# A four-layer graph network on one Trainium2 core: layer 0's graph part issued from a planned list, its second weight product in seven-product form

## The chip, the cores and the metric

The kernel runs on one core of one Trainium2 chip. The core has five engines with an instruction queue each: TensorE (PE in the profile, with its weight loads shown apart as PEld), VectorE (DVE), ScalarE (ACT), GpSimd (POOL) and SyncE (SP), which here only starts DMAs. Each engine takes its instructions in order, and waits for the others through semaphores. The metric is the device time of one execution in microseconds, the median of several runs. All arithmetic is float32.

## The reference

The input `x` is 128 sequences of 64 rows with 256 features, so 8192 rows; `adj` is one 64x64 matrix for all sequences. Four layers follow each other, each as `x = x + layer(relu(layernorm(x)))`. The change is in layer 0 alone:

```python
h = jnp.maximum(_layernorm(x, axis=-1), 0.0)
# the graph part of layer 0
h = jax.nn.relu(jnp.einsum('ts,bsh->bth', adj, h @ Wg0 + bg0))
h = jax.nn.relu(jnp.einsum('ts,bsh->bth', adj, h @ Wg1 + bg1))
# then, for p = 1..4, an LSTM over windows of p rows rewrites every p-th row of h
x = x + h
```

Layer 1 is a graph product with two weight products and batch norms, layer 2 three weight products on three parts of `adj`, layer 3 attention within each sequence. They stay as they are.

## The kernel before, in words

The 8192 rows are cut into 16 supertiles of 512 rows (`SUP`; `Q` = 4 blocks of `P` = 128 rows, two sequences each). `graph_part(s)` (from L277) is a generator that does one supertile in five stages, with a `yield` between them:

- load `xt` (one DMA of 512 KB, four of 128 KB for the first supertile), layer norm and ReLU to `h`: statistics on DVE (`norm_of`, L181 to L185), a power on POOL in their midst (L184), four activations on ACT (L191)
- `aggregate` to `g0`: 8 matmuls of 128x128 against the block-diagonal adjacency `adjT_bd` (L207), two PSUM copies on DVE (L208)
- the first weight product: 8 matmuls with 256 moving columns (L303), two additions of the bias on DVE (L305), one ReLU on ACT (L307), to `h1`
- `aggregate` to `g1`: as above, from `h1`
- the second weight product: for each of two output halves `o` two matmuls with 512 moving columns (L314), one bias operation on DVE (L317), one ReLU on ACT (L320), which writes transposed features into `hT`, the input of the LSTM

`pipelined(..., 1)` starts a new supertile every round and runs one stage of each live supertile a round, the youngest supertile first. The order of issue on each engine is just the order of these calls: in each round the load and layer norm of one supertile, `g0` of the one before, the first weight product of the next older, then `g1`, then the second weight product. Nothing is reordered afterwards (`manual_schedule`); an engine's queue is the order of the program.

Other work rides on the same stages: `row_sums` with supertile 0 (L129 to L133), `more_constants` with supertile 2 (weights and biases by DMA), `adjacencies` with 4, `normalize` with 7, and `weight_sums` (four POOL additions on LSTM weights, L267 to L270) with 9.

The LSTM that follows is written in another way. Its `at(t, fn)` puts every instruction with a due time by hand into a list `events`, and the list is sorted and issued. Its products use a seven-product form of a 2x2 block product (a Winograd form of Strassen): weights as `A11, A12, A21, A22` with the sums `S1` to `S4` made once, the moving side as two halves of columns with the sums `tx`, and results added up in PSUM banks named a, b and c. Its tiles come from the pools `lg`, `lh0` and `lh1`, opened after the graph part's pools `pa` and `pax` are closed, in the same memory. A pool opened with `reuse_waits="tile"` waits tile by tile for the older users of its memory; without it, it waits for all of them together. PSUM has 8 banks in one rotating pool (`bank()`).

Of the kernel before, what the change touches and what calls it, by code (L numbers as in the profile page):

```python
# [9 lines left out]
F32 = mybir.dt.float32  # L10
AF = mybir.ActivationFunctionType
ALU = mybir.AluOpType
AX = mybir.AxisListType

P = 128
# [5 lines left out]
def kernel(ctx: ExitStack, tc: tile.TileContext, a: dict, out: bass.AP):  # L21
# [48 lines left out]
    def bank():  # L70
        return psum.tile([P, 512], F32, tag="ps", name="ps")
# [11 lines left out]
    def weight(name, src, pool=const, queue=nc.sync):  # L83
        k, m = src.shape
        return load_const(name, src.rearrange("(c p) m -> p c m", p=P), [P, k // P, m], pool, queue)
# [21 lines left out]
    con = {}  # L107

    def more_constants():
        con["wg1"] = weight("wg1", a["Wg1"], first)  # L110
        con["bg1"] = load_const("bg1", a["bg1"], [P, KC], first)
        con["bih"] = load_const("bih", a["bih"], [P, NL, NM])
        con["bhh"] = load_const("bhh", a["bhh"], [P, NL, NM])
        con["bn1"] = load_const("bn1", a["bn1"], [P, 3, HC])
        con["bn2"] = load_const("bn2", a["bn2"], [P, 3, KC])
        con["w1"] = weight("w1", a["W1T"])
# [10 lines left out]
    def row_sums():  # L127

        nc.vector.reduce_sum(rs_col, adj_bd, axis=AX.X)  # L129
        nc.vector.tensor_scalar_mul(rsb, bg0, rs_col)  # L130
        ps = bank()
        nc.tensor.matmul(ps[:, :P], ones, adjT_bd, start=True, stop=True)
        nc.vector.tensor_copy(rs_row, ps[:, :P])  # L133

    def adjacencies():

        nc.vector.tensor_add(lbias, con["bih"], con["bhh"])


        scr = first.tile([P, P], F32, tag="scr", name="scr")  # L140
        nc.vector.tensor_add(scr, adj_bd, ident)
        nc.vector.reduce_sum(deg[:, 0:1], scr, axis=AX.X)
        nc.vector.tensor_mul(scr, scr, ident)
        nc.vector.reduce_sum(deg[:, 1:2], scr, axis=AX.X)
        nc.vector.tensor_add(ahT, adjT_bd, ident)
        nc.vector.reduce_sum(deg[:, 2:3], ahT, axis=AX.X)
        nc.vector.tensor_add(deg[:, 0:1], deg[:, 0:1], deg[:, 2:3])
        nc.vector.tensor_sub(deg[:, 0:1], deg[:, 0:1], deg[:, 1:2])
        nc.gpsimd.tensor_tensor(deg[:, 3:4], deg[:, 0:1], mhalf[:, 0:1], ALU.pow)
        dd = first.tile([P, P], F32, tag="dd", name="dd")  # L150
        nc.vector.tensor_scalar_mul(dd, ident, deg[:, 3:4])


        nc.vector.tensor_mul(adj3[:, 0, :], adjT_bd, ident)
        nc.gpsimd.affine_select(adj3[:, 1, :], adjT_bd, pattern=[[-1, P]], base=0,
                                channel_multiplier=1, compare_op=ALU.is_gt, fill=0.0)
        nc.gpsimd.affine_select(adj3[:, 2, :], adjT_bd, pattern=[[1, P]], base=0,
                                channel_multiplier=-1, compare_op=ALU.is_gt, fill=0.0)


        nc.gpsimd.affine_select(smask, adj_bd, pattern=[[-1, P]], base=0, channel_multiplier=1,
                                compare_op=ALU.is_ge, fill=NEG)
        nc.vector.memset(smask[T:P, 0:T], NEG)
        return dd

    def normalize(dd):
        ps = bank()
        nc.tensor.matmul(ps[:, :P], ones, dd, start=True, stop=True)
        nc.vector.scalar_tensor_tensor(ahT, ahT, deg[:, 3:4], ps[:, :P], op0=ALU.mult, op1=ALU.mult)


    def bcast_q(t):
        return t[:, None, :].to_broadcast([P, Q, t.shape[1]])
# [20 lines left out]
    def layernorm_relu(pool, src, tag="ln_h", bufs=None):  # L194

        rn = norm_of(pool, src)
        h = pool.tile([P, Q, D], F32, tag=tag, name=tag, bufs=bufs)
        normalize_relu(h, src, rn)
        return h

    def aggregate(pool, h, mT, tag, bufs=None):

        g = pool.tile([P, KC, SUP], F32, tag=tag, name=tag, bufs=bufs)
        for c in range(KC):
            p_ = bank()
            for q in range(Q):
                nc.tensor.matmul(p_[:, ts(q, P)], h[:, q, ts(c, P)], mT, start=True, stop=True)  # L207
            nc.vector.tensor_copy(g[:, c, :], p_)  # L208
        return g
# [18 lines left out]
    def graphs(s, c):  # L228

        v = hT[s // SG][:, c, :].rearrange("p (t b) -> p b t", b=GB)  # L230
        b = (s % SG) * (SUP // T)
        return v[:, b : b + SUP // T, :]

    def pipelined(gens, skew, live=()):


        gens, live, r = list(gens), list(live), 0
        while gens or live:
            if gens and r % skew == 0:
                live.insert(0, gens.pop(0))  # L240
            live = [g for g in live if next(g, "end") != "end"]
            r += 1
# [14 lines left out]
    def load_lstm(src, tag, pool):  # L257
        w = pool.tile([P, 7, 4, P], F32, tag=tag, name=tag)
        v = src.rearrange("(c p) (g h m) -> h c p g m", p=P, g=4, m=P)
        for h in range(2):  # L260
            for c in range(2):
                nc.sync.dma_start(w[:, 2 * h + c], v[h, c])
        return w

    def weight_sums(w):
        g = nc.gpsimd
        g.tensor_add(w[:, S1], w[:, A21], w[:, A22])  # L267
        g.tensor_sub(w[:, S2], w[:, S1], w[:, A11])
        g.tensor_sub(w[:, S3], w[:, A11], w[:, A21])
        g.tensor_sub(w[:, S4], w[:, A12], w[:, S2])  # L270

    GATES = (("i", 0, AF.Sigmoid), ("g", 2, AF.Tanh), ("f", 1, AF.Sigmoid), ("o", 3, AF.Sigmoid))


    with tc.tile_pool(name="pa", bufs=2) as pa, tc.tile_pool(name="pax", bufs=3) as pax:

        def graph_part(s):  # L277
            xt = pax.tile([P, Q, D], F32, tag="xt", name="xt")
            if s == 5:
                wih0.append(load_lstm(a["WihT"][0], "wih", lwa))  # L280
            for q in range(Q if s == 0 else 1):
                part = slice(q, q + 1 if s == 0 else Q)
                nc.sync.dma_start(xt[:, part, :], x_r[s, :, part, :])
            if s == 2:
                more_constants()
            h = layernorm_relu(pa, xt)
            if s == 0:
                row_sums()
            if s == 4:
                made.append(adjacencies())  # L290
            if s == 7:
                normalize(made[0])
            if s == 9:
                weight_sums(wih0[0])
            yield
            g0 = aggregate(pa, h, adjT_bd, "g0")
            yield
            h1 = pa.tile([P, Q, D], F32, tag="h1", name="h1")
            for q2 in range(0, Q, 2):
                p_ = bank().rearrange("p (q d) -> p q d", q=2)  # L300
                for q in range(2):
                    for c in range(KC):
                        nc.tensor.matmul(p_[:, q, :], g0[:, c, ts(q2 + q, P)], wg0[:, c, :],  # L303
                                         start=(c == 0), stop=(c == KC - 1))
                nc.vector.tensor_add(h1[:, q2 : q2 + 2, :], p_,  # L305
                                     rsb[:, None, :].to_broadcast([P, 2, D]))
            nc.scalar.activation(h1, h1, AF.Relu)  # L307
            yield
            g1 = aggregate(pa, h1, adjT_bd, "g1")
            yield  # L310
            for o in range(KC):
                p_ = bank()
                for c in range(KC):
                    nc.tensor.matmul(p_, con["wg1"][:, c, ts(o, P)], g1[:, c, :],  # L314
                                     start=(c == 0), stop=(c == KC - 1))
                t = pa.tile([P, SUP], F32, tag="h2", name="h2")
                nc.vector.scalar_tensor_tensor(  # L317
                    t.rearrange("p (q n) -> p q n", q=Q), bcast_q(rs_row), con["bg1"][:, o : o + 1],
                    p_.rearrange("p (q n) -> p q n", q=Q), op0=ALU.mult, op1=ALU.add)
                nc.scalar.activation(graphs(s, o), t.rearrange("p (b t) -> p b t", t=T), AF.Relu)  # L320
            yield

        wih0, made = [], []
        pipelined(map(graph_part, range(NS)), 1)
    graph_weights.close()


# [45 lines left out]
        yield  # L373


    lg = lstm.enter_context(tc.tile_pool(name="lg", bufs=1))

    lh1 = lstm.enter_context(tc.tile_pool(name="lh1", bufs=1))
    even_state = ExitStack()
    lh0 = even_state.enter_context(tc.tile_pool(name="lh0", bufs=1))  # L380
    events = []

    def at(t, fn, *args):
        events.append((t, len(events), fn, args))
# [514 lines left out]
```

## Time and profile before

| what | value |
|---|---|
| median of 6 runs | 1917.87 us (1914.57 to 1918.6) |
| the profiled execution: its own time / its span | 1916.72 us / 1915.0 us |
| mean granted TensorE clock | 0.996 |
| graph part: first aggregation to first LSTM product | 8.68 us to 182.65 us of the span |
| DMA over the span | 54.28 MB, mean 28 GB/s |

The table of slices (40 equal parts of the span) shows which engine is full where; a digit is the busy share in tenths, 9 meaning 90% or more. The first four columns are the graph part:

```profile
## 2 busy tenths in 40 slices
PE   7999999999999999999999999999999899999998
PEld 6776444444445666665444444555444788888886
DVE  6775777734546445445633334688786456565554
ACT  3554666534435435434533333444574333333332
POOL 1110322443424432322522224533152211111110
```

All times below are from the start of the span. In the profile a float32 matmul is two records, each with its weight load; records overlap, so a record's duration is longer than the distance from one to the next.

### The profile page before, as it was taken

What the parts mean: (1) busy time and instruction counts of PE and PEld (TensorE: products, weight loads), DVE (VectorE), ACT (ScalarE), POOL (GpSimd) and SP (SyncE); (2) the same over time, 40 slices, a digit from 0 to 9 for tenths busy, and PEclk for the clock granted to TensorE, in tenths of its full rate; (3) what the DMA queues carried; (4) which work ended last, traced back from release to release, by engine and by line L of the source; (5) the groups of instructions that cost most, each with busy time, mean ns of one, the idle gap of its engine ahead of it and who ended that gap; (6) DMA issues with size and microseconds to landing.
All of it is one profiled execution on the core that took longest, in us unless ns stands there. A gap on an engine that the chain in (4) does not pass through costs nothing.

```text
span 1915.0 us, 18932 instructions
## 1 busy us (share of the span) xinstructions
PE 1883.5 (98%) x6932; PEld 1147.5 (60%) x6932; DVE 1098.8 (57%) x2144; ACT 849.1 (44%) x1429; POOL 552.2 (29%) x363
## 2 busy tenths in 40 slices
PE   7999999999999999999999999999999899999998
PEld 6776444444445666665444444555444788888886
DVE  6775777734546445445633334688786456565554
ACT  3554666534435435434533333444574333333332
POOL 1110322443424432322522224533152211111110
PEclk9999999999999999999999999999999899999999
DMA  4110000100001000000000001233200001110111
GB/s 137 56 55 1 1 1 10 34 0 0 0 1 45 1 1 0 1 1 23 0 0 1 1 0 44 77 110 110 64 0 31 25 23 45 45 45 23 44 34 45
DMA packets 49469, 54.28 MB, mean 28 GB/s; under 512 B 3040, under 2 KB 44768, under 8 KB 49376
## 3 DMA queue, kind: packets, MB, share of 16 engines
q1 hardware_dynamic: 48640, 52.61, 8.8%
q8 instruction: 55, 0.90, 0.2%
q10 hardware_dynamic: 736, 0.46, 0.1%
q14 instruction: 38, 0.31, 0.1%
HBM read 36.28 MB, written 16.78 MB: 28 GB/s over the span
## 4 chain that ended last, share of the span: by engine, by line
PE 95%; DVE 2%; POOL 1%; ACT 1%; issue 1%; DMA 0%; SPq 0%; DVEq 0%; ACTq 0%; POOLq 0%
PE ps L449 34%; PE ps L455 19%; PE ps L796 9%; PE ps L365 6%; PE ps L684 5%; PE ps L207 4%; PE ps L303 3%; PE ps L822 3%; PE ps L314 3%; PE ps L814 3%; PE ps L783 2%; PE ps L830 1%; PE ps L217 1%; PE ps L851 1%; PE ps L807 1%
## 5 line engine op out<-in xcount | busy, mean ns | idle before, releaser
L471 DVE TENSOR_TENSOR gate<-gate,ps 128x512 f32<-128x512 f32 (+2 forms) x378 | 223.9, 619 | 446.4 <-PE ps L455 367.0
L449 PE MATMUL ps<-tx,wih 128*128 128x512 f32 (+2 forms) x1008 | 446.5, 542 | 3.1 <-issue 1.2
L449 PE MATMUL ps<-hT,wih 128*128 128x512 f32 (+2 forms) x756 | 338.5, 541 | 0.0
L449 PEld LDWEIGHTS ps<-tx,wih 128*128 128x128 f32 x1008 | 190.6, 190 | 193.0 <-issue 133.4
L474 ACT COPY gate<-ps 128x512 f32<-128x512 f32 (+2 forms) x252 | 134.2, 533 | 379.1 <-PE ps L455 325.2
L467 ACT ACTIVATE gate<-gate,lbias 128x512 f32<-128x512 f32 (+2 forms) x252 | 216.7, 860 | 158.0 <-DVE gate L471 158.0
L455 PE MATMUL ps<-h,whh 128*128 128x512 f32 (+2 forms) x576 | 256.6, 527 | 0.0
L449 PEld LDWEIGHTS ps<-hT,wih 128*128 128x128 f32 x756 | 143.6, 190 | 141.6 <-issue 79.9
L184 POOL TENSOR_TENSOR ln_rn<-ln_rn,mhalf 128x4 f32<-128x4 f32 x64 | 64.7, 1011 | 514.4 <-DVE ln_rn L183 514.4
L455 PE MATMUL ps<-th,whh 128*128 128x512 f32 (+2 forms) x432 | 192.5, 527 | 0.0
L796 PE MATMUL ps<-wl,ag 128*128 128x256 f32 x768 | 169.5, 381 | 0.0
L455 PEld LDWEIGHTS ps<-h,whh 128*128 128x128 f32 x576 | 109.4, 190 | 100.2 <-issue 76.5
L494 POOL TENSOR_TENSOR gate<-gate 128x1024 f32<-128x1024 f32 (+2 forms) x36 | 71.9, 2019 | 304.7 <-ACT gate L467 304.7
L796 PEld LDWEIGHTS ps<-wl,ag 128*128 128x128 f32 x768 | 145.7, 191 | 19.4
L191 ACT ACTIVATE ln_h<-x,ln_rn 128x256 f32<-128x256 f32 x128 | 66.4, 589 | 201.7 <-DVE ln_rn L185 201.7
L494 POOL TENSOR_TENSOR cell<-gate 128x1024 f32<-128x1024 f32 (+2 forms) x36 | 79.4, 2228 | 200.1 <-ACT gate L467 200.1
L455 PEld LDWEIGHTS ps<-th,whh 128*128 128x128 f32 x432 | 82.1, 190 | 75.2 <-issue 57.4
L365 PE MATMUL ps<-ag,w 128*128 128x512 f32 x256 | 112.3, 592 | 0.0
L494 POOL TENSOR_TENSOR cell<-gate,cell 128x1024 f32<-128x1024 f32 (+2 forms) x32 | 65.1, 2052 | 109.3 <-ACT gate L467 109.3
L474 DVE COPY gate<-ps 128x512 f32<-128x512 f32 (+2 forms) x126 | 78.5, 623 | 20.9 <-PE ps L455 20.8
L467 ACT ACTIVATE gate<-ps,lbias 128x512 f32<-128x512 f32 (+2 forms) x126 | 79.5, 631 | 3.9 <-PE ps L455 1.0
L499 ACT ACTIVATE gate<-cell 128x1024 f32<-128x1024 f32 (+2 forms) x72 | 68.1, 952 | 29.4 <-POOL cell L494 29.4
(193 smaller groups left out, 2571.9 us busy)
## 6 DMA issues: line engine op xcount, KB each, us to landing
xt<-in_x_dram SPq DMA_DIRECT2D x31, 512.0 KB, 4.3
x1d<-xt SPq DMA_DIRECT2D x16, 512.0 KB, 3.0
x<-x1d SPq DMA_DIRECT2D x16, 512.0 KB, 4.4
out_dram<-x SPq DMA_DIRECT2D x16, 512.0 KB, 3.2
wih<-in_WihT_dram SPq DMA_DIRECT2D x16, 256.0 KB, 4.6
whh<-in_WhhT_dram SPq DMA_DIRECT2D x12, 256.0 KB, 5.0
wl<-in_W_dram SPq DMA_DIRECT2D x3, 256.0 KB, 2.8
wqkv<-in_Wqkv_dram SPq DMA_DIRECT2D x1, 768.0 KB, 6.4
```

The source lines that it names most:

```text
L191: nc.scalar.activation(h[:, q, :], src[:, q, :], AF.Relu, bias=rn[:, 1, q : q + 1], scale=rn[:, 0, q : q + 1])
L207: nc.tensor.matmul(p_[:, ts(q, P)], h[:, q, ts(c, P)], mT, start=True, stop=True)
L365: nc.tensor.matmul(p_, con["w1"][:, c, ts(o, P)], ag[:, c, :], start=(c == 0), stop=(c == KC - 1))
L449: nc.tensor.matmul(wide(p_[:, :N]), wih[0][:, OF[k], gi, :], x_, start=first_, stop=(j == 0), skip_group_check=True)
L455: nc.tensor.matmul(p_[:, :N], whh[0][:, OF[k], gi, :], h_, start=False, stop=True, skip_group_check=True)
L467: nc.scalar.activation(to, r[bank_][:, :N] if bank_ else to, fn, bias=lbias[:, l, m : m + 1])
L471: nc.vector.tensor_add(slot(n, hc), slot(n, hc), r[bank_][:, :N])
L474: op(slot(n, hc), r[bank_][:, :N])
L494: fn(*((t["G"] if isinstance(t, dict) and "G" in t else st["c"])[:, n, :, : st["N"]] for t in tiles))
L499: nc.scalar.activation(o_, c, AF.Tanh)
L684: nc.tensor.matmul(banks[name], w2[:, OF[j], k, :], x_, start=(new and k == 0), stop=(k == 1), skip_group_check=True)
L796: nc.tensor.matmul(p_[:, q, :], ag[:, c, k, ts(q2 + q, P)], wl2[k][:, c, :], start=(n == 0), stop=(n == 3 * KC - 1))
```

## The change

`graph_part(s)` becomes a function that puts its instructions, each with a due time counted from `10 * s` us, into a list; the list is sorted by due time and issued, as the LSTM's is. The order of a round on each engine is now set by these due times, not by stages. With it:

- The second weight product of supertiles 0 to 14 takes seven products of 256 moving columns (`product`) in place of four of 512. Each half of 256 columns is one column of blocks. The sums of the weights `wg1` are made once on POOL (from a loaded copy `wg1p`), the sums of the data on POOL for each supertile (`sums`, four subtractions of 128x256), the results are taken from PSUM by seven DVE operations of 128x256 (`begun` four times, `add` three times). Supertile 15 keeps the four products (`direct`).
- PSUM copies of the aggregations move from DVE to ACT (`aggregated`), and the ReLU of `h1` is split into two of 128x512 (`relu1`).
- `g1` of a supertile comes a round later than `g0` with its first weight product, and the second weight product another round later. In supertile 0 the layer norm is done in two halves.
- `adjacencies` is cut into pieces at different due times; some of its DVE work moves to POOL. The load of the first LSTM weights comes after two more loads of `xt`; `weight_sums` of them is spread over a round.
- `lg`, `lh0` and `lh1` get `reuse_waits="tile"`.

The diff, cut to its core:

```diff
     def more_constants():
-        con["wg1"] = weight("wg1", a["Wg1"], first)
+        con["wg1p"] = weight("wg1p", a["Wg1"], first)
+        con["wg1"] = first.tile([P, 7, P], F32, tag="wg1", name="wg1")
+        for o in range(2):
+            for c in range(2):
+                nc.gpsimd.tensor_copy(con["wg1"][:, 2 * o + c, :], con["wg1p"][:, c, ts(o, P)])
...
         def graph_part(s):
...
+            t0, v = ROUND * s, {}
+
+            def at(t, fn, *args):
+                events.append((t0 + t, len(events), fn, args))
...
+            def root(qs):
+                rn = v["rn"][:, 0, qs]
+                nc.vector.tensor_scalar_add(rn, v["mv"][:, qs, 1], EPS)
+                nc.gpsimd.tensor_tensor(rn, rn, mhalf[:, : qs.stop - qs.start], ALU.pow)
+
+            def shift(qs):
+                nc.vector.scalar_tensor_tensor(v["rn"][:, 1, qs], v["mv"][:, qs, 0], -1.0,
+                                               v["rn"][:, 0, qs], op0=ALU.mult, op1=ALU.mult)
...
+            def aggregated(g, c):
+                nc.scalar.copy(v[g][:, c, :], v["p", g, c])
...
+            def sums(k):
+                if k == 0:
+                    v["t"] = pa.tile([P, 4, HALF], F32, tag="t", name="t")
+                t = v["t"]
+                nc.gpsimd.tensor_sub(t[:, k], *((g_(0, 1), g_(0, 0)), (g_(1, 1), t[:, 0]),
+                                                (g_(1, 1), g_(0, 1)), (g_(1, 0), t[:, 1]))[k])
+
+            def product(name, j):
+                new = ("q", name) not in v
+                if new:
+                    v["q", name] = bank()[:, :HALF]
+                x_ = (g_(0, 0), g_(1, 0), g_(1, 1), *(v["t"][:, k] for k in (3, 0, 1, 2)))[j - 1]
+                nc.tensor.matmul(v["q", name], con["wg1"][:, OF[j], :], x_, start=new,
+                                 stop=(name, j) in (("a", 4), ("b", 3), ("c", 2)), skip_group_check=True)
+
+            def begun(o, n, name):
...
+                nc.vector.scalar_tensor_tensor(
+                    v["h2"][:, o, ts(n, HALF)].rearrange("p (q n) -> p q n", q=2),
+                    rs_row[:, None, :].to_broadcast([P, 2, P]), con["bg1"][:, o : o + 1],
+                    v["q", name].rearrange("p (q n) -> p q n", q=2), op0=ALU.mult, op1=ALU.add)
+
+            def add(o, n, name):
+                h2 = v["h2"][:, o, ts(n, HALF)]
+                nc.vector.tensor_add(h2, h2, v["q", name])
...
+            if s == 0:
+                halves = ((slice(0, 2), -8.6), (slice(2, 4), -7.4))
...
+            else:
+                halves = ((slice(0, 4), -11.9),)
+                at(-15.2, new_norm)
+                for q in range(Q):
+                    at((-15.1, -14.5, -13.1, -12.5)[q], stats, q)
+            for qs, t in halves:
+                at(t, root, qs)
+                at(t + 1.4, shift, qs)
+                for q in range(qs.start, qs.stop):
+                    at((2.7 - ROUND if s == 1 else t + 1.5) + 0.6 * (q - qs.start), relu, q)
+            late, end = 0, s == NS - 1
+            for c in range(KC):
+                at(late + 0.86 + 1.75 * c, aggregate0, "g0", "h", c)
+                at(late + 0.87 + 1.75 * c, aggregated, "g0", c)
+            for k in range(2):
+                at(late + 6.56 + 1.72 * k, weigh, k)
+                at(late + 8.3 + 1.75 * k, weighed, k)
+                at(late + 8.9 + 1.75 * k, relu1, k)
+            late += ROUND
+            for c in range(KC):
+                t = (0.86, 2.6)[c] if end else 4.35 + 0.89 * c
+                at(late + t, aggregate0, "g1", "h1", c)
+                at(late + t + 0.01, aggregated, "g1", c)
+            if end:
+                for o in range(KC):
+                    at(late + 5.2 + o, direct, o)
+                return
+            for k in range(4):
+                at(late + 7.2 + 0.7 * k, sums, k)
+            late += ROUND
+            for t, name, j in ((0, "c", 2), (0.43, "a", 1), (1.75, "b", 5), (2.18, "a", 6),
+                               (3.5, "b", 3), (3.93, "a", 7), (6.1, "a", 4)):
+                at(late + t, product, name, j)
+            at(late + 0.5, begun, 0, 0, "c")
+            at(late + 0.9, add, 0, 0, "a")
+            at(late + 2.3, begun, 1, 1, "b")
+            at(late + 2.7, begun, 0, 1, "a")
+            at(late + 4.0, add, 0, 1, "b")
+            at(late + 4.4, add, 1, 1, "a")
+            at(late + 5.0, relu2, 0)
+            at(late + 6.6, begun, 1, 0, "a")
+            at(late + 7.1, relu2, 1)
...
+            if s == 2:
+                at(-20.5, more_constants)
+                at(-9.5, lambda: weight_sums(con["wg1"]))
...
-        pipelined(map(graph_part, range(NS)), 1)
+        for s in range(NS):
+            graph_part(s)
+        for _, _, fn, args in sorted(events, key=lambda e: e[:2]):
+            fn(*args)
...
-    lg = lstm.enter_context(tc.tile_pool(name="lg", bufs=1))
+    lg = lstm.enter_context(tc.tile_pool(name="lg", bufs=1, reuse_waits="tile"))
```

In a list of due times, `weigh` and `weighed` are the matmuls and the bias additions of the first weight product (before: L303 and L305), `relu` and `relu2` the activations of L191 and L320, `stats` the statistics of L181 and L182.

## The prediction

> **What bounds the kernel now.** I read the page's busy shares and chain of waits first, then the table of stretches for the graph part, then the order of time on TensorE, and last the order of time of all engines where TensorE stands still.
>
> ```profile
> PE 1883.5 (98%) x6932; PEld 1147.5 (60%) x6932; DVE 1098.8 (57%) x2144; ACT 849.1 (44%) x1429; POOL 552.2 (29%) x363
> ...
> PE 95%; DVE 2%; POOL 1%; ACT 1%; issue 1%; DMA 0%; SPq 0%; DVEq 0%; ACTq 0%; POOLq 0%
> ```
>
> TensorE carries 95% of the chain that ends last. The stretches say the same of the graph part, after a poor start (engines in the order PE, PEld, DVE, ACT, POOL, then granted clock and DMA share):
>
> ```profile
> 0.00:27.34 27.34, 17.43 (x83) 15.58 (x84) 15.26 (x53) 9.28 (x17) 4.93 (x12) 0.94 0.69 201
> 27.34:182.65 155.31, 155.31 (x819) 118.92 (x818) 109.04 (x254) 75.63 (x98) 18.42 (x20) 1.00 0.14 41
> ```
>
> From 27.34 us on, TensorE has no gap until the LSTM. So there only fewer TensorE columns can help, and before it only an earlier start. TensorE in order of time, one round and the head:
>
> ```profile
> 8.68 3.82 PE L207 MATMUL ps<-adjT_bd,ln_h 128*128 128x128 f32 x16 [3.80 <-ACT ln_h L191]
> 14.49 3.98 PE L207 MATMUL ps<-adjT_bd,ln_h 128*128 128x128 f32 x16 [1.99 <-ACT ln_h L191]
> 18.26 4.00 PE L303 MATMUL ps<-wg,g 128*128 128x256 f32 x16
> ...
> 27.34 1.95 PE L207 MATMUL ps<-adjT_bd,h 128*128 128x128 f32 x16
> ...
> 97.35 1.95 PE L207 MATMUL ps<-adjT_bd,h 128*128 128x128 f32 x16
> 99.13 3.60 PE L314 MATMUL ps<-g,wg 128*128 128x512 f32 x8
> 102.57 1.95 PE L207 MATMUL ps<-adjT_bd,ln_h 128*128 128x128 f32 x16
> 104.35 3.62 PE L303 MATMUL ps<-wg,g 128*128 128x256 f32 x16
> 107.81 1.95 PE L207 MATMUL ps<-adjT_bd,h 128*128 128x128 f32 x16
> ```
>
> The distances of these starts are the prices: an aggregation 1.78 us, the second weight product 3.44, the first 3.46 for 8 matmuls of 256 columns, so 0.43 each. A round is 10.46 us.
>
> **Seven products.** Per supertile 7 x 0.43 = 3.01 us replace 3.44; the row for 128x256 is L303, the same shape with a new weight each time, so no other price is needed. Saved: 0.43 x 15 = 6.45 us. A round is then 1.78 + 3.46 + 1.78 + 3.01 = 10.03 us.
>
> What these products need must hide in 10.03 us. Vector: seven PSUM operations of 128x256 (nearest rows 475 ns for L854, 484 for an addition of 128x320; distance some 0.42) make 2.9; with statistics 2.1, two bias additions 1.3 and two small ones 0.3 it is 6.6. Scalar: four copies of 0.585, four layer norm activations at distance 0.52, two halves of 0.63, two writes of 1.1 make 7.9. GpSimd: four subtractions at 0.725 (128x256 in layer 1's weights) and the power 1.01 make 3.9. None is full; what can fail is the order.
>
> I followed one round in queue order, counting from product c, with 0.27 us from a matmul's end to its reader (L317 starts that late) and 0.05 from a reader to TensorE. Product a6 may only start (due 2.19) when `add` has read bank a. In front of that `add` on Vector stand `begun`, the second `weighed`, and the `shift` of a layer norm, which waits for the power on GpSimd, which stands behind `sums` 0 and 1. These wait for the copies of `g1`: the second ends at 7.7 (Scalar does an output ReLU of 1.1 between the two), `sums` 1 at 8.68, the power at 9.7, the shift could start at 9.75.
>
> Here a rule speaks against the change. A blocked shift is in the trace, where the LSTM weight sums run on GpSimd; elsewhere it takes 0.16:
>
> ```profile
> 86.15 1.26 POOL L267 TENSOR_TENSOR wih<-wih 128x512 f32<-128x512 f32 x1
> 86.22 1.22 DVE L185 SCALAR_TENSOR_TENSOR ln_rn<-ln_mv,ln_rn 128x4 f32<-128x4 f32 x1 [1.21 <-POOL ln_rn L184]
> ...
> 87.35 1.28 DVE L208 COPY g<-ps 128x512 f32<-128x512 f32 x2
> ...
> 87.49 1.27 POOL L268 TENSOR_TENSOR wih<-wih 128x512 f32<-128x512 f32 x1
> ```
>
> [...] The shift [...] comes 0.04 us after the power, when `sums` 2 has begun: it ends at 10.45, not 9.9. By the free row the `add` would be past without any wait; by the rule, `weighed` runs from 10.42 (its matmuls are in at 10.30), `begun` from 11.02, `add` from 11.4 to 11.8, and a6 is due at 12.2. I take the rule, since the row shows it, and it leaves about 0.33 us: **no stall**. Copies and bias additions[...] kept their 1.28 for two beside GpSimd. The unknown bounds: nothing, up to a shift that waits for `sums` 2 and 3 at a contended price (below).
>
> **The head.** Before, the first weight product waits behind the second supertile's aggregation, which waits for its layer norm; it starts at 18.26. In the new order it stands directly behind the first aggregation, so it starts when its weights land (issued 4.27, 8.3 us to landing: 12.6). Halving the first layer norm starts the aggregation about 1 us earlier, which that landing swallows. But the next steps hang on Vector's queue: statistics of supertile 1 start when its x lands (10.08), shift 13.64, row sums to 14.65, statistics of supertile 2 to 16.85; only then the first bias addition (17.0), power, shift (18.25, or 18.65 behind the `wg1` sums), second addition to 19.35. Scalar then does two layer norms, the ReLU half (20.4), and around two more the copies of `g0` of supertile 1 to 22.65. So TensorE stands about 0.9 us before the rest of `g1` and 0.9 before the second supertile's weight product, which runs 22.7 to 26.2. By then TensorE has done 3 aggregations and 2 weight products, as much as before at 27.34. **Gain 1.1.** GpSimd's four `wg1` copies, four sums of 128x128 and the moved adjacency pieces (0.3 to 0.4 each) lie before `g1` is there. The SP queue's order changes only where xt goes ahead of LSTM weights, needed 130 us later.
>
> [...]
>
> ```profile
> 15.00:16.00 1.00, 1.00 (x5) 0.71 (x5) 0.93 (x5) 0.91 (x2) 0.00 (x0) 0.81 1.03 382
> 16.00:17.00 1.00, 1.00 (x6) 1.00 (x6) 0.93 (x5) 0.00 (x0) 0.00 (x0) 0.50 1.00 354
> ```
>
> [...] after 1.99 us of idleness and a thin start it was 0.50 until 19, about 3.4 us at half speed, 1.7 us lost. By the row my two gaps could cost that 1.7 again[...]. They are half as long, with work between: I take nothing and keep 1.7 for a rival.
>
> **The last round and the LSTM's start.** Supertile 15's `g1` follows its weight product at once; bias addition and ReLU end at 1.6 where TensorE is ready at 1.3: 0.35, with 0.05 before `direct`, is 0.4 lost. At the hand-over before:
>
> ```profile
> 182.65 1.88 PE L449 MATMUL ps<-hT,wih 128*128 128x512 f32 x4
> ...
> 184.81 0.69 DVE L411 TENSOR_TENSOR tx<-hT 128x512 f32<-128x512 f32 x1 [1.14 <-ACT hT L320]
> ...
> 185.71 1.95 PE L449 MATMUL ps<-tx,wih 128*128 128x512 f32 x4 [1.18 <-issue]
> ```
>
> `tx` waits for the last ReLU, as its pool waits for all of `pa`. With waits by tile it follows Vector's own last step: a gap of 0.5. But three output ReLUs (3 x 1.1) now end late on Scalar, ahead of the LSTM's first copy of bank a, which its third product needs: 0.9 more. So 1.35 in place of 1.18, **0.2 lost**; the new waits gain nothing.
>
> **The sum.** Head -1.1; stage -6.45 + 0.4 = -6.05; hand-over +0.2: about **-7.0 us**. The LSTM and what follows keep their order on TensorE, which is full there, so it comes through. The profiled execution took 1916.72 us (1.7 more than its span), so 1909.7 by its own time; it lies 1.15 below the median of the runs, 1917.87. On the median: 1910.9.
>
> **Rivals.**
> - *As summed*, 1910.9, 0.66; its own range 1909 to 1913.
> - *A cold clock in the head*: 1.7 us back, 1912.6. For it the 0.50 above; against it the shorter gaps. 0.14.
> - *A better head*: Vector's steps tighter than I laid them, both gaps of 0.9 closed: 1909.1. 0.06.
> - *The shift waits for two sums*: [...] 0.73 later, less the 0.33 of slack is 0.4 a round, times 14 is 5.6: 1916.5. Against it: the blocked shift above ended before L268 began. 0.08.
> - *[...] it is slower*: as the last, but GpSimd also at its contended price, 1718 ns in place of 1267 for 128x512 in layer 1 (L674, L668's kind), so 0.98 for a sum: `sums` 1 ends 0.25 later, two sums take 1.96, the shift comes 1.47 later than I have it, 1.14 a round beyond the slack, 16 us: 1926.9. It passes the old time from 0.83 us of lateness on. Against it: the four weight sums within this stage kept 1.26 to 1.28. 0.06.
>
> **How the numbers follow.** The first three are faster by over 0.2% (3.8 us, about what a measurement of this kernel tells from no change): 0.86. Within it the fourth, 0.08; slower 0.06. The range takes the first three and some 2 us of spread, as the runs of before show: 1907 to 1915.
>
> **What would show it.** Right: rounds of 10.03 us on TensorE, the first of the seven products near 26.2, the LSTM's first near 175.5, shifts of 0.7 us. Wrong: a gap before a6 in each round; a granted clock of 0.5 after 19 us; the first weight product later than 12.6; Scalar's copies late before `weigh`.

## The result, and the profile after

| | kernel before | changed kernel |
|---|---|---|
| median | 1916.76 us (36 runs, 1914.48 to 1918.75) | 1911.89 us (16 runs, 1909.83 to 1914.32) |
| profiled execution: time / span | 1916.72 / 1915.0 us | 1910.25 / 1908.4 us |

The ratio is 0.9976, with a 95% interval of 0.9969 to 0.9982: the change wins 4.9 us, between 3.4 and 5.9. The sum said 7.0. The page of the changed kernel, its busy shares and the shares of its chain of waits:

```profile
PE 1875.3 (98%) x7022; PEld 1161.0 (61%) x7022; DVE 1091.6 (57%) x2155; ACT 881.7 (46%) x1509; POOL 598.4 (31%) x434
...
PE 94%; DVE 3%; ACT 1%; POOL 1%; issue 1%; DMA 1%; SPq 0%; DVEq 0%; ACTq 0%; POOLq 0%
```

TensorE is still what everything waits for, busy for 8 us less; Scalar and GpSimd each carry 33 to 46 us more. Where the time went is in the stretches of the changed kernel, cut at the first of the seven products and at the LSTM's first product (columns as before):

```profile
0.00:24.95 24.95, 15.67 (x83) 13.93 (x83) 13.07 (x50) 12.57 (x23) 10.89 (x29) 1.00 0.61 178
24.95:177.54 152.59, 150.04 (x910) 135.81 (x908) 103.76 (x266) 104.55 (x169) 58.80 (x75) 1.00 0.17 49
177.54:1908.40 1730.86, 1709.54 (x6033) 1011.30 (x6031) 974.79 (x1840) 764.58 (x1317) 528.68 (x331) 1.00 0.08 24
```

At both first cuts TensorE has done the same work as before at 27.34 and at 182.65. So the head gives 2.39 us and the stage 155.31 - 152.59 = 2.72. The third stretch is 1.49 shorter than before (1732.35), with the same instructions on TensorE: the granted clock between 1480 and 1530 us (the column before the DMA share) was 0.90 in the execution of before, 0.97 in this one, and 0.90 again in another profiled execution of the changed kernel, in this order:

```profile
1480.00:1530.00 50.00, 43.31 (x223) 36.44 (x223) 26.46 (x76) 14.33 (x30) 12.12 (x8) 0.90 0.09 32
1480.00:1530.00 50.00, 45.67 (x278) 39.22 (x279) 28.10 (x74) 19.03 (x40) 11.20 (x8) 0.97 0.06 22
1480.00:1530.00 50.00, 46.78 (x270) 40.19 (x271) 26.39 (x70) 17.20 (x35) 11.08 (x7) 0.90 0.07 22
```

In that other execution the third stretch took 1732.2, as before the change, so these 1.5 us are no part of it. What is left, 5.1 us, is near the 4.9 of the medians.

The stage had to be 6 us shorter, and in its busy TensorE time there are 2.55 us missing: it stands still. TensorE's starts of `product` c2 are 10.05 us apart in every round but four: 10.20 in the first, 0.22 more where the matmul of `normalize` stands, 11.97 in the one from 55.25 and 11.01 in the one from 107.64. All engines in a normal round, in order of time (start, duration, engine, line, operation):

```profile
117.25 1.01 POOL L316 TENSOR_TENSOR ln_rn<-ln_rn,mhalf 128x4 f32<-128x4 f32 x1 [0.24 <-DVE ln_rn L315]
...
118.22 0.72 POOL L362 TENSOR_TENSOR t<-g 128x256 f32<-128x256 f32 x1
118.29 0.68 DVE L319 SCALAR_TENSOR_TENSOR ln_rn<-ln_mv,ln_rn 128x4 f32<-128x4 f32 x1 [0.40 <-POOL ln_rn L316]
118.65 1.03 PE L370 MATMUL ps<-g,wg 128*128 128x256 f32 x4
118.89 0.68 DVE L347 TENSOR_TENSOR h<-ps,rsb 128x512 f32<-128x512 f32 x1
...
119.49 0.47 DVE L377 SCALAR_TENSOR_TENSOR h<-rs_row,bg,ps 128x256 f32<-128x256 f32 x1
...
120.06 0.42 DVE L384 TENSOR_TENSOR h<-h,ps 128x256 f32<-128x256 f32 x1
120.41 1.03 PE L370 MATMUL ps<-t,wg 128*128 128x256 f32 x4
```

The reader sees the chain of the prediction: the power (L316), the shift that is held 0.68 us by the third sum (L319 beside L362; in the run below that has no sums on GpSimd it takes 178 ns on average), `weighed` (L347), `begun` (L377), `add` (L384), which ends at 120.48. Product a6 is the second half of the last line's group, due 0.43 after 120.41, at 120.84: 0.36 us after the end of `add`. Not all of this is free. Where a6 does wait, in the two rounds below, it starts 0.15 after the end of `add` (59.29 after 59.14, 110.72 after 110.57), so 0.21 us of it is slack. Now the round from 55.25 us:

```profile
52.97 0.66 DVE L152 TENSOR_TENSOR deg<-deg 128x1 f32<-128x1 f32 x1
53.55 0.41 DVE L310 BATCH_NORM_STATS2 ln_st<-xt 128x6 f32<-128x256 f32 x1
...
55.91 1.01 POOL L316 TENSOR_TENSOR ln_rn<-ln_rn,mhalf 128x4 f32<-128x4 f32 x1 [2.30 <-DVE ln_rn L315]
...
56.95 0.68 DVE L319 SCALAR_TENSOR_TENSOR ln_rn<-ln_mv,ln_rn 128x4 f32<-128x4 f32 x1 [0.52 <-POOL ln_rn L316]
...
58.72 0.42 DVE L384 TENSOR_TENSOR h<-h,ps 128x256 f32<-128x256 f32 x1
...
59.29 0.67 PE L370 MATMUL ps<-t,wg 128*128 128x256 f32 x2 [1.69 <-DVE h L384]
```

Nine Vector operations of `adjacencies` (the sums of the degrees among them) stand before the statistics of a layer norm. The power starts 0.66 us after c2 here (55.91 against 55.25), 1.40 before c2 in the normal round; a6 waits 1.69 us. The round grows by 1.92, 0.23 more than this gap: a record (0.60) outlasts the distance to the next start (0.43), and the matmul behind the gap is longer (0.67). And the round from 107.64:

```profile
105.95 1.27 POOL L277 TENSOR_TENSOR wih<-wih 128x512 f32<-128x512 f32 x1
105.98 1.27 DVE L315 TENSOR_SCALAR ln_rn<-ln_mv 128x4 f32<-128x4 f32 x1
...
107.33 1.01 POOL L316 TENSOR_TENSOR ln_rn<-ln_rn,mhalf 128x4 f32<-128x4 f32 x1
...
108.38 0.68 DVE L319 SCALAR_TENSOR_TENSOR ln_rn<-ln_mv,ln_rn 128x4 f32<-128x4 f32 x1 [0.54 <-POOL ln_rn L316]
...
110.72 0.67 PE L370 MATMUL ps<-t,wg 128*128 128x256 f32 x2 [0.73 <-DVE h L384]
```

One addition on the LSTM weights holds the little operation ahead of the power (L315, otherwise 0.17 us) for 1.27 us, and a6 waits 0.73. The addition also stands ahead of the power in GpSimd's own queue and ends at 107.22, so the power could hardly have started before 107.3 even with L315 free; no run here tells the two apart.

### The profile page after: what moved, and what is told of

The parts are those of the page before. It is cut to its first block, busy times and chain, and to the rows that moved or that the text cites. A ratio compares the mean times of both kernels' runs of the same rounds, so it can differ in the third digit from the quotient of the medians.

```text
span 1908.4 us, 19347 instructions
## 1 busy us (share of the span) xinstructions
PE 1875.3 (98%) x7022; PEld 1161.0 (61%) x7022; DVE 1091.6 (57%) x2155; ACT 881.7 (46%) x1509; POOL 598.4 (31%) x434
## 4 chain that ended last, share of the span: by engine, by line
PE 94%; DVE 3%; ACT 1%; POOL 1%; issue 1%; DMA 1%; SPq 0%; DVEq 0%; ACTq 0%; POOLq 0%
PE ps L599 34%; PE ps L605 19%; PE ps L946 9%; PE ps L515 6%; PE ps L834 5%; PE ps L972 3%; PE ps L964 3%; PE ps L331 3%; PE ps L341 2%; PE ps L933 2%; PE ps L370 2%; PE ps L980 1%; PE ps L217 1%; PE ps L1001 1%; PE ps L227 1%; PE ps L957 1%
## 5 line engine op out<-in xcount | busy, mean ns | idle before, releaser
L194 POOL TENSOR_TENSOR ln_rn<-ln_rn,mhalf 128x4 f32<-128x4 f32 x48 | 48.5, 1010 | 389.5 <-DVE ln_rn L193 389.5
```

## The experiments

My theory: one-time work that stands ahead of a layer norm's power eats this slack, and the shift in Vector's queue carries the delay on to a6. The rivals: the gaps belong to something else in those rounds; or the gain never came from the products but from the order. Since the head moves from run to run (the first seven-product matmul starts between 23.21 and 25.42 us in five traces with the same head), I compare the stage, from the first seven-product matmul to the LSTM's first product. In the changed kernel it takes 152.59 us.

**The weight additions moved.**

```diff
-                    at(0.4 + 2.5 * k, lambda k=k: weight_sum(wih0[0], k))
+                    at((1.6, 3.0, 11.6, 13.0)[k], lambda k=k: weight_sum(wih0[0], k))
```

> The four GpSimd additions on the LSTM weights are put where GpSimd idles (directly behind a supertile's last sum) instead of one of them ahead of a layer norm's power. My theory (one-time work ahead of the power delays shift, weighed and the add that product a6 waits for): the gap of 0.73 us before a6 near 110 us goes, that round falls from 11.0 to 10.05 us, the first LSTM product starts near 176.6 instead of 177.54 us. Rival (the gap belongs to that round's own steps, for instance a PSUM bank that comes late, wherever the additions stand): the gap stays, the start stays at 177.5.

Measured: the gap is gone, that round is 10.05 us; the stage takes 176.20 - 24.58 = 151.62, 0.97 less. L315 is 169 ns on average again, in place of 243. Median 1910.61, ratio 0.9964 (0.9951 to 0.9976).

**The degrees spread.**

```diff
-                at(5.0, adjacencies)
-                at(11.5, degrees_root)
-                at(13.3, lambda: made.append(degrees()))
+                pieces = adjacencies()      # now a generator, one operation a step
+                for k in range(9):
+                    at(6.1 + 10 * (k // 2 - 1), next, pieces)
+                at(41.5, degrees_root)
+                at(43.3, lambda: made.append(degrees()))
```

(`normalize` follows two rounds later.)

> The nine Vector operations of the degrees, which stood together in one round, go two to a round into Vector's free place before the third begun; the root and the scaling follow later. My theory: the gap of 1.69 us before a6 near 59 us goes, that round falls from 11.97 to 10.05 us, no other round grows, the first LSTM product starts near 175.6 us. Rival (the round is late by the root on GpSimd between the sums and the add, not by Vector's queue): the gap moves along with the root to the later round, and the start stays at 177.5.

Measured: the gap of 1.69 is gone and comes back nowhere, the gap of 0.73 (0.74 here) stays; the stage takes 176.14 - 25.42 = 150.72, 1.87 less. The rival that the root moves the gap along falls. Median 1909.44, ratio 0.9961 (0.9947 to 0.9974).

**The shift on GpSimd**, so that nothing in Vector's queue waits for GpSimd's power, while all one-time work stays where it was:

```diff
                 nc.vector.tensor_scalar_add(rn, v["mv"][:, qs, 1], EPS)
+                nc.vector.tensor_scalar_mul(v["rn"][:, 1, qs], v["mv"][:, qs, 0], -1.0)
                 nc.gpsimd.tensor_tensor(rn, rn, mhalf[:, : qs.stop - qs.start], ALU.pow)
+                nc.gpsimd.tensor_mul(v["rn"][:, 1, qs], v["rn"][:, 1, qs], rn)
...
             def shift(qs):
-                nc.vector.scalar_tensor_tensor(v["rn"][:, 1, qs], v["mv"][:, qs, 0], -1.0,
-                                               v["rn"][:, 0, qs], op0=ALU.mult, op1=ALU.mult)
+                pass
```

> Vector only makes the negative mean, and GpSimd multiplies it behind its power, so that Vector's queue holds no operation that waits for GpSimd. My theory: what carries the delay from GpSimd to TensorE is this shift in Vector's queue. Without it both gaps before a6 (1.69 and 0.73 us) go or fall below 0.3, all rounds are 10.05 us, the first LSTM product starts near 174.9 us, and the kernel is some 2.5 us faster than the changed kernel. Rival (the delay goes through the late statistics and Scalar's activations to TensorE, and not through the shift): the gaps stay within 0.3 us.

Two groups of this kernel's profile (mean duration in ns after the busy time), and the one gap left:

```profile
L315 DVE TENSOR_SCALAR ln_rn<-ln_mv 128x4 f32<-128x4 f32 x15 | 3.7, 244 | 1.3
...
L318 POOL TENSOR_TENSOR ln_rn<-ln_rn 128x4 f32<-128x4 f32 x15 | 3.0, 201 | 1.2
```

```profile
58.13 0.67 PE L371 MATMUL ps<-t,wg 128*128 128x256 f32 x2 [0.63 <-DVE h L385]
```

L315 is held as before (244 ns on average), the power is as late as before, and yet the second gap is gone: it was the shift that carried it. Of the first gap 0.63 stays, twice what I expected at most: those nine operations fill Vector's own queue, and `add` is late without any shift (it starts 2.41 us after c2, against 1.41 in the normal round above). The stage takes 175.42 - 25.01 = 150.41, 2.18 less. Median 1909.11, ratio 0.9957 (0.9944 to 0.9969).

**More load on GpSimd.**

```diff
+            def extra():
+                x_ = pa.tile([P, SUP], F32, tag="extra", name="extra", bufs=1)
+                nc.gpsimd.tensor_sub(x_, v["g1"][:, 1, :], v["g1"][:, 0, :])
...
+            at(late + 8.0, extra)           # in each round, between sums 1 and the power
```

> One more GpSimd subtraction of 128x512 (1.27 us, its result unused) in each round, between the second sum and the power. GpSimd is then busy for about 5.4 of 10 us. My theory (slack of about 0.35 us on the way power, shift, weighed, begun, add): a6 waits some 0.7 to 0.9 us in each of 15 rounds, rounds are 10.8 to 11.0 us, the time is 10 to 13 us above the changed kernel's, some 6 us above the kernel before. Rival (GpSimd's free 6 us a round hide it): within 1 us of the changed kernel.

```profile
L315 DVE TENSOR_SCALAR ln_rn<-ln_mv 128x4 f32<-128x4 f32 x15 | 14.5, 965 | 0.7
```

```profile
108.16 0.67 PE L370 MATMUL ps<-t,wg 128*128 128x256 f32 x2 [0.73 <-DVE h L384]
```

Now the operation ahead of the power is held in nearly every round (965 ns on average), and the power itself stands behind the added subtraction in GpSimd's queue. Nearly every round has a gap of 0.7 before a6 and takes 11.0 us, and the stage grows by 12.0 to 164.56. Median 1924.19, 1.0035 of the kernel before (1.0021 to 1.0048). GpSimd's idle time counts for nothing here; the place of the added work in the order does.

**Four products in the planned list**: the list without seven products, so without sums on GpSimd and with two bias operations on Vector.

```diff
-            for k in range(4):
-                at(late + 7.2 + 0.7 * k, sums, k)
...
+            for o in range(KC):
+                at(late + 1.75 * o, four, o)        # two matmuls of 512 columns
+                at(late + 2.3 + 1.7 * o, biased, o)
+                at(late + 5.0 + 2.1 * o, relu2, o)
```

> The planned list with the four products of 512 columns for all supertiles: no sums on GpSimd, two bias operations on Vector in place of seven. My theory (list and head give 2.4 us, the seven products 6.45 us less 3 us of gaps): rounds of 10.48 us without gaps, the first LSTM product near 181 us, so some 1.5 to 2.5 us below the kernel before and some 3 us above the changed one. Rival (all of the gain comes from the order): as fast as the changed kernel, first LSTM product near 177.5.

Measured: rounds of 10.46 us without a gap, the stage 180.83 - 25.43 = 155.40, as in the kernel before. Median 1915.7, ratio 0.9993 (0.9985 to 1.0001): 0.85 below the kernel before, less than I expected, and its interval, from a gain of 2.9 to a loss of 0.2, includes no gain. Its first LSTM product (180.83) is as expected, 1.82 before the old one, all of it won in the head. So the order alone is worth 0.9 by the medians and 1.8 by the trace; the stage is shorter only with the seven products (152.59).

**Seven products in the old order**: the stages as before, the sums on GpSimd behind the second aggregation, and in the last stage all seven products with their seven Vector operations between them.

```diff
             g1 = aggregate(pa, h1, adjT_bd, "g1")
+            tt = pa.tile([P, 4, HALF], F32, tag="t", name="t")     # four sums on GpSimd
             yield
-            for o in range(KC):                                    # four products
...
+            product("c", 2)
+            product("a", 1)
+            begun(0, 0, "c")
+            add(0, 0, "a")
+            product("b", 5)
+            product("a", 6)
...
```

> The kernel before, in its old stage order, with its second weight product in seven-product form (all supertiles, sums on GpSimd at the end of the stage before). My theory (a bank that collects several products must be read by Vector in between, and only other matmuls in between hide that): TensorE waits 1 to 2 us in each supertile against 0.43 saved, so 8 to 25 us slower than the kernel before. Rival (the product form pays whatever the order): some 5 us faster than the kernel before.

```profile
83.54 0.42 DVE L345 TENSOR_TENSOR h<-h,ps 128x256 f32<-128x256 f32 x1
...
84.11 0.67 PE L334 MATMUL ps<-t,wg 128*128 128x256 f32 x2 [0.58 <-POOL t L323]
84.61 0.59 PE L334 MATMUL ps<-g,wg 128*128 128x256 f32 x2
84.82 0.48 DVE L338 SCALAR_TENSOR_TENSOR h<-rs_row,bg,ps 128x256 f32<-128x256 f32 x1 [0.46 <-PE ps L334]
...
85.45 0.67 PE L334 MATMUL ps<-t,wg 128*128 128x256 f32 x2 [0.24 <-POOL t L323]
86.15 0.42 DVE L345 TENSOR_TENSOR h<-h,ps 128x256 f32<-128x256 f32 x1 [0.33 <-PE ps L334]
...
86.72 0.67 PE L334 MATMUL ps<-t,wg 128*128 128x256 f32 x2 [0.60 <-DVE h L345]
```

TensorE waits three times in each supertile, 1.42 us together by the gaps against 0.43 saved; by the starts the seven products take 5.16 us in place of 3.01. The profile puts two of the three down to GpSimd's sums, but each matmul also starts 0.15 us after Vector's read of the bank ends (83.96, 85.30 and 86.57), the same distance as in the changed kernel's two late rounds. So earlier sums alone could hardly have helped; no run has them. A matmul behind a gap is also longer (0.67 in place of 0.60), and a round takes 12.15 us (84.11 to 96.26) in place of 10.46, which is 27 us over 16 supertiles. The first supertile has gaps of 1.78 and 3.23 us besides, and behind the second, from 44.53 to about 52 us, its matmuls take 1.06 and 1.19 us in place of 0.59 and 0.67, an aggregation 3.35 in place of 1.95. The median is 1951.83, ratio 1.0185 (1.0170 to 1.0201): 35 us slower, more than the 8 to 25 that I gave. In this kernel the product form pays only with other matmuls between its steps.

**The LSTM pools waiting as before.**

```diff
-    lg = lstm.enter_context(tc.tile_pool(name="lg", bufs=1, reuse_waits="tile"))
+    lg = lstm.enter_context(tc.tile_pool(name="lg", bufs=1))
```

(and likewise `lh1` and `lh0`.)

> The changed kernel with the LSTM pools as before, waiting for all users of the older pools together. My prediction said that the waits by tile gain nothing, for Scalar's copy of bank a is late anyway: the first data sum then waits for the last output activation, TensorE has one gap of about 1.9 us in place of 0.21 and 0.65, and what follows is later by at most 1 us; I expect +0.5 to 1.0 us. Rival: no difference at all within 0.2 us, or over 1.5 us.

The hand-over of the changed kernel, of all engines:

```profile
177.54 1.88 PE L599 MATMUL ps<-hT,wih 128*128 128x512 f32 x4
...
178.80 0.68 DVE L561 TENSOR_TENSOR tx<-hT 128x512 f32<-128x512 f32 x1
179.63 1.10 PE L599 MATMUL ps<-tx,wih 128*128 128x512 f32 x2 [0.21 <-DVE tx L561]
...
180.54 0.69 DVE L561 TENSOR_TENSOR tx<-hT,tx 128x512 f32<-128x512 f32 x1 [1.06 <-ACT hT L400]
...
181.38 1.10 PE L599 MATMUL ps<-tx,wih 128*128 128x512 f32 x2 [0.65 <-DVE tx L561]
```

and of this kernel, TensorE and a stretch of the windows:

```profile
181.65 2.48 PE L599 MATMUL ps<-tx,wih 128*128 128x512 f32 x4 [2.00 <-DVE tx L561]
```

```profile
184.00:186.00 2.00, 2.00 (x4) 0.93 (x3) 0.67 (x2) 0.59 (x1) 0.00 (x0) 0.50 0.00 0
```

One gap of 2.00 us in place of 0.21 and 0.65, as expected, but behind it the granted clock falls to 0.50 for a while, so in this trace the hand-over costs 2.6 us more and not 1.1 (from the LSTM's first product to its third group of products on `hT`, 10.81 against 8.20). The median is 1913.01, ratio 0.9984 (0.9976 to 0.9992) against 0.9976: about a microsecond, and the intervals overlap.

**All three together**: weights moved, degrees spread, shift on GpSimd; measured twice, the second time beside the changed kernel on the same chip.

> The changed kernel with the weight additions moved, the degrees spread and the shift on GpSimd. My theory: no gap before a6 in any round, 15 rounds of 10.05 us, first LSTM product near 174.5 us, so about 3 us faster than the changed kernel and about 8 us faster than the kernel before. Rival (the gaps overlap other losses): not below 176.5 us.

> The changed kernel as it is, beside the next one on the same chip. The first LSTM product within 0.6 us of 177.5; the head moves by some tenths from run to run with the landing of the first transfers, the two gaps before a6 (1.69 and 0.73 us) stand again. About 4.9 us below the kernel before.

> The version with the weight additions moved, the degrees spread and the shift on GpSimd, on the same chip as the changed kernel. My theory, from the first LSTM product at 173.7 against 177.5 us: 3 to 4 us faster than the changed kernel. Rival (what is won in the graph part is lost behind it): within 1.5 us of it.

Measured: no gap in any round, the stage takes 149.55 and 149.54 us; medians 1908.92 and 1907.59, ratios 0.9959 (0.9946 to 0.9971) and 0.9955 (0.9942 to 0.9967). The changed kernel beside the second: 1911.81, ratio 0.9978 (0.9968 to 0.9988), its gaps 1.69 and 0.73 again, but its LSTM started at 175.80, not within 0.6 of 177.54: the head was 1.74 shorter, the stage 152.59 to the hundredth. So this version is 4.2 us faster than the changed kernel beside it, a little more than expected, and 7.6 and 8.9 us faster than the kernel before. The stage accounts for 3.05 of the 4.2; where the rest comes from, no trace shows.

## Why the prediction came out as it did

The time lay in the range and the direction was right; the gain was put at 7.0 and is 4.9. That it came this close is in part luck: the stage gave 3.3 us less than forecast, and the head and the hand-over gave 1.6 more, so that two errors offset each other in part. With the head as forecast the time would have been about 1913, still in the range.

- **Seven products at 0.43, a round of 10.03 us**: right. Rounds without one-time work are 10.05.
- **The held shift, 0.33 us of slack, no stall**: that a sum would hold the shift was my estimate from one row of the trace of before (1.22 us at 86.22, beside an addition of 1.26). It was right for a normal round (shifts of 631 ns on average, against 178 in the run without sums, and no stall), and the slack a little smaller than forecast, 0.21, as 0.15 passes from the end of `add` to TensorE where I took 0.05. The step that failed is the conclusion "no stall", drawn for all rounds from one. The list also issues one-time work, and I priced none of what it puts with supertiles 4 and 9: the nine Vector operations of `adjacencies`, and the additions on the LSTM weights, which the list of changes names as spread over a round. They cost 1.9 and 1.0 us; both are taken back by the two experiments that move only them. With so little slack, every operation that joins a round had to be followed along the same chain.
- **The head, 1.1 us**: the mechanism (Vector's queue of statistics) was right, the size too small. It gave 2.4 in this trace, 1.7 more in the second one, and of the kernel before there is only one trace to compare with; the x of supertile 1 was there at 9.63 in place of 10.08, and the steps behind it were tighter. TensorE had one gap of 1.14 us in it where I had two. The clock stayed at 1.00 from 8 us on, so the price that I took for the clock, nothing, an estimate, held here. It need not: in the run with more load on GpSimd, whose head is the same up to there, TensorE stood still for 2.22 us until the weights of the first weight product had landed (6.3 us after their issue in this trace), and that product took 5.38 us, against 3.69 in six runs where it waited 0.59 to 1.70 us for them; the first seven-product matmul came at 26.36. So the 1.7 us of the rival with a cold clock in the head were lost in that trace.
- **The last round, 0.4 us**: right; from the last c2 to the LSTM's first product 8.65, against 1.78 + 3.01 + 3.44 and the 0.4 lost, 8.63.
- **The hand-over, 0.2 lost, and "the new waits gain nothing"**: the two gaps are 0.86 us together against 1.18, and from the first to the next `hT` group the LSTM takes 4.77 against 4.85. In the new order, with three output activations at the end, the old waits give one gap of 2.00: the new waits do gain 1.1 us there by the trace, though the medians' intervals overlap.
- **The two rivals of a shift held for longer**: both fall. The sums kept their 0.73 (means of 733 and 730 ns), a shift was held by one sum and not by two, and a6 waited in two rounds of 15, not in each.

Added up: head 1.3 more than forecast, stage 3.3 less (2.9 of it the two kinds of one-time work, the rest some 0.02 a round and 0.15 in the first), hand-over 0.3 better: 5.2 by the trace.

## What to carry to other kernels

In a list of due times, find the operation with the least slack in a normal round, then take every one-time instruction that the list puts into some round and follow it along that same chain; a sum of busy times says nothing about it. An operation that waits for another engine is dear in the queue of the engine that must release TensorE: moving a 128x4 operation to the engine that it waits for won back 2.2 us here. A product form that collects several products in one bank pays where other matmuls lie between its steps (0.43 us a supertile here), and costs three gaps a supertile where none do (1.42 us together).

## What was not expected of the hardware

Like the shift, the small operation ahead of the power is held beside GpSimd: L315 (128x4, a scalar added) took 1.27 us beside a GpSimd addition of 128x512, and 965 ns on average where a GpSimd subtraction of that size stood ahead of each power, against 0.17 elsewhere; with the additions moved its mean fell from 243 to 169 ns. Why it is held, no run here tells. And TensorE's clock fell to 0.50 behind a gap of 2.00 us in the kernel with the old pool waits, as it did behind 1.99 us in the kernel before. Behind 2.22 us in the run with more load on GpSimd the weight product took 5.38 us in place of 3.69; behind 1.82 us in that run four matmuls of 128x128 took 1.05 us as elsewhere, and behind 1.69 and 1.14 us in the changed kernel the clock stayed at 1.00. The length of a gap does not decide alone. The kernel before and the first trace of the changed kernel have the same gap of 3.22 us, up to 1508.31 and 1502.94 us: behind it the clock was 0.50 until 1514 us in the one and stayed at 1.00 in the other, and the stretch from the LSTM's first product to the end took 1732.35 and 1730.86 us. In six more traces that stretch took 1730.8 to 1730.9 us twice, with a mean clock of 0.99 from 1400 to 1560 us as in the first of the changed kernel, and 1732.2 to 1732.6 us four times, the second trace of the changed kernel among these. What decides is not shown.
